# A two-layer network on one core: layer 1's last attention product and feed forward by token tile, five weight-quantising operations instead of one, and a new set of scheduling tables

## Chip, cores and metric

The kernel runs on one NeuronCore of a Trainium2 chip. The time is that of the device for one launch, in microseconds (us), as the median of several executions; with one core there is no slowest one to choose. The engines are TensorE (PE in the profile: matmuls, with its weight loads listed as PEld), VectorE (DVE), ScalarE (ACT), GpSimd (POOL) and SyncE (SP). SyncE does no arithmetic here: it issues all the DMA transfers, also the transposing ones.

## The reference, cut to what matters

The input `x` is 64 sequences of 64 tokens with 256 features each, so 4096 tokens; `ctx_2048` has the same shape. Six blocks are added to `x` one after the other, each from a layer-normalised `x`:

```python
x = x + L0_attn(layernorm(x))          # 16 heads, 4 shared K/V heads, 128 wide, rotary, causal
x = x + L0_xattn(layernorm(x), ctx)    # 8 heads; features attend to features
x = x + L0_ffn(layernorm(x))           # base product + one of 8 low-rank experts for each token
x = x + L1_attn(layernorm(x))          # 16 heads of 16, one shared K/V head, causal
x = x + L1_xattn(layernorm(x), ctx)    # 16 heads of 128, RMS-normalised q and k
x = x + L1_ffn(layernorm(x))           # 8 bit SwiGLU, 704 wide
```

The two blocks that the change touches, cut to their core:

```python
# L1_xattn
q = rms_norm(x @ q_w + q_b, nq_s);  k = rms_norm(ctx @ ki_w + ki_b, nki_s);  v = ctx @ vi_w + vi_b
out = softmax(q k^T / sqrt(128)) v            # per head, 64 x 64 in each sequence
return out @ o_w + o_b

# L1_ffn
def _quant_dequant(v):                        # per row
    scale = max(max|v| / 127, 1e-8)
    return clip(round(v / scale), -127, 127) * scale
gate, up = split(_quant_dequant(x) @ _quant_dequant(w_gate_up)^T)
h = silu(gate) * up
return _quant_dequant(h) @ _quant_dequant(w_down)^T
```

## The kernel before, in words

**Tiling.** The 4096 tokens go in 16 groups of 256 (`GT`). A group is held as an array `xt` of 128 partitions by 2 token tiles by 256 features; index `j` counts the token tiles. Layer 0 (called phase a: the blocks a0, x0, f0) is done for a group, the result goes to DRAM (`mid`), and layer 1 (phase b: a1, x1, f1) reads it back. Phase a of later groups and phase b of earlier ones are in flight together around the middle of the run.

**The order.** No loop of the text sets the order in which the engines get their instructions. The text of each block records operations: `s.o(engine, cost, reads, writes, function)`, and `s.alt` where two engines may do it. One operation can issue several instructions of one engine, and those then stand together. When all are recorded, a planner (`Sched.plan`) goes through them as a list scheduler on its own cost figures. An operation has a due time: a target that comes from the phase's pace (`PACE`, `SHIFT`), plus an entry of `LEAD` for the block and the name of the tile, plus an entry of `FINE` for its place in the group. Among the operations that could start on an engine at about the same time (`EPS`), the one with the earliest due time is taken. `HOLD` is added to the due time of a TensorE operation that would change the tile mode (the part of the array that a matmul uses: 128x128, 128x64, 128x32 or 32x128), `PEN` counts against a choice where VectorE would take an operation that another engine could take, `WINDOW` is how many groups of each phase may be open, `SPACE` sets the least distance between the score steps of x0, and `TMIN` the earliest starts of setup operations. The planned order is emitted as straight code, engine by engine: each engine then runs its own list in order, and waits at the semaphores of what it needs. A planned order is thus fixed when the kernel is built; the planned times are not.

**Memory.** Tiles come from pools by size: `B` (8 banks of PSUM, 2 KB a partition), `k4` (6 buffers of 4 KB), `k2` (67 of 2 KB), `k1` (6 of 1 KB), `sm` (10 small ones).

**Lines that the change and the prediction speak of.**

- Helpers: `layer_norm` (L555 statistics, L557 aggregation, L562 and L566 small GpSimd steps, L569 the normalising on ScalarE); `dma_T` (L578, a transposing DMA of a whole tile); the three-term product of split f16 numbers (L430 to L432); `softmax_rows` (L625 to L655: maxima, differences, exponentials, sums, the split `phl`).
- a0: query products `q_ps`, sums of squares `ss` (L881), scores `s_ps` (L933) with a mask and scale step (L935, L937), `po` products from the transposed `pt` (L689), the split `ohl` (L694, L696), output product `acc`.
- x0: `stack_rows` sends rows through DRAM into `ovl` (the issues `hl_d` and `ovl`), `xs_ps` scores (L1033), maxima `xmx` (L1040), `mx_ps` and `mneg` (the maxima are transposed and sent through DRAM as one more row), `xt_ps` scores again in the other orientation (L1067), exponentials `xpt` (L1074), `xo_ps` (L1083), the sum at L1113.
- f0: `f0o_ps` (L1167). a1: `q1st` rows sent through DRAM, `s_ps` (L1312), `pT` transposes and the context product (L1327).
- x1 (`l1_xattn`): q and k products `qk_ps` with biases (L1650), scores `s_ps` (L1662). Its heads go in two halves of eight; for each, `value_block` makes `vn` = context times a product of value and output weights (`vn_ps` L1541; ScalarE takes the high half L1546, VectorE the low half L1548), and `attend_rows` multiplies the probabilities into it.
- `attend_rows`: for both token tiles a transposing DMA of `phl` to `pt` and 24 matmuls into one PSUM tile `acc` of 128 x 2 x 256 (L1564); then one VectorE instruction adds `acc` times a scale to the whole `xt` (L1568).
- f1 weights (`l1_ffn_prep`, once, at the start of phase b): five chunks, each a load `f_w` (L1693), one VectorE operation of six instructions (L1699 the row maximum, L1677 and L1678 the scale and its reciprocal, L1701 the multiplication, L1702 and L1703 the rounding by adding and subtracting a large number), TensorE transposes `fw_ps` (L1712), a ScalarE copy `f_t` (L1715) and stores to DRAM (L1719).
- f1 (`l1_ffn`): layer norm, row maximum `f1am` (L1764), scale `f1sx` (L1765) and its reciprocal `f1ix` (L1766), each one instruction for both token tiles; rounding per token tile (L1768, L1770); one transposing DMA for both, `xqT`; then per token tile four products `gu_ps` of two matmuls (L1784) scaled out of PSUM by VectorE (L1786), ScalarE's `sig` (L1789), GpSimd's gate product (L1791), the second quantisation (L1799 to L1812), the transposing DMA `hqT`, the product `f1o_ps` (L1819), its scaling (L1822) and GpSimd's addition into `xt` (L1825). One DMA writes the group's output (L2081).

Of the kernel before, what the change touches and what calls it, by code (L numbers as in the profile page):

```python
# [11 lines left out]
BF16 = mybir.dt.bfloat16  # L12
# [7 lines left out]
D = 256  # L20
# [16 lines left out]
HOLD = 965  # L37
# [1514 lines left out]
def attend_rows(e, xt, phl, vn, uo):  # L1552


    nc, s = e.nc, e.s
    acc = s.T("B", [128, 2, D], name="acc")
    for j in range(2):
        pt = s.T("k2", [128, 8, 128], F16, name="pt")
        dma_T(e, phl[j], pt, lambda t: t.rearrange("p a h l -> p (a h l)"))

        def f(t, h0, l0, h1, l1, o, j=j):
            for n, (p, a, c) in enumerate((p, a, c) for p in range(4) for a, c in ((0, 0), (0, 1), (1, 0))):
                for b in range(2):
                    nc.tensor.matmul(o[64 * b:64 * b + 64, j, :], t[:, 4 * a + p, 64 * b:64 * b + 64],  # L1564
                                     ((h0, l0), (h1, l1))[b][c][:, p, :], start=(n == 0), stop=(n == 11))
        s.o("PE", 12 * 110, [pt] + list(vn[2 * j] + vn[2 * j + 1]), [acc.sub(j)], f, tile=3)
    s.o("DVE", c_dve(512, 1), [acc, uo], [xt],
        lambda a, u, x: nc.vector.scalar_tensor_tensor(x, a, u, x, ALU.mult, ALU.add))  # L1568
# [112 lines left out]
def l1_ffn_prep(e, I):  # L1681
# [4 lines left out]
    for nm, src, nr, n, per in (("gu", I["w_gu"], 11, 256, 4), ("dn", I["w_dn"], 2, 704, 1)):  # L1686
# [3 lines left out]
        for a0 in range(0, nr, per):  # L1690
# [7 lines left out]
            def f(t, am, iv, sc, b, a0=a0, na=na, n=n):  # L1698
                nc.vector.tensor_reduce(am, t, AX.X, ALU.max, apply_absolute_value=True)  # L1699
                row_scale(nc, sc[:, a0:a0 + na], iv, am)  # L1700
                nc.vector.tensor_tensor(t, t, bc(iv, 2, n), ALU.mult)  # L1701
                nc.vector.tensor_scalar(t, t, MAGIC, None, ALU.add)  # L1702
                nc.vector.tensor_scalar(b, t, MAGIC, None, ALU.subtract)  # L1703
            s.o("DVE", 3.2 * na * n + 500, [t], [am, iv, sc.sub(a0), b], f)
# [50 lines left out]
def l1_ffn(e, xt):  # L1755
# [3 lines left out]
    xh = layer_norm(e, xt, 1.0)  # L1759
    am, sx, ix = (s.T("sm", [128, 2], name="f1" + n) for n in ("am", "sx", "ix"))  # L1760
    xq = s.T("k1", [128, 2, D], BF16, name="xq")

    V = nc.vector
    s.o("DVE", c_dve(512), [xh], [am], lambda x, am: V.tensor_reduce(am, x, AX.X, ALU.max, apply_absolute_value=True))  # L1764
    s.o("DVE", Port(130), [am], [sx], lambda am, sx: V.tensor_scalar(sx, am, 1.0 / 127, 1e-8, ALU.mult, ALU.max))  # L1765
    s.o("DVE", Port(140), [sx], [ix], lambda sx, ix: V.reciprocal(ix, sx))  # L1766
    for j in range(2):
        s.o("DVE", c_dve2(256, 1), [ix], [xh.sub(j)], lambda ix, x, j=j: V.tensor_scalar(  # L1768
            x[:, j, :], x[:, j, :], ix[:, j:j + 1], MAGIC, ALU.mult, ALU.add))
        s.o("DVE", c_dve2(256), [xh.sub(j)], [xq.sub(j)], lambda x, q, j=j: V.tensor_scalar(  # L1770
            q[:, j, :], x[:, j, :], MAGIC, None, ALU.subtract))
    xqT = s.T("k1", [128, 4, 128], BF16, name="xqT")
    dma_T(e, xq, xqT, lambda t: t.rearrange("p j n -> p (j n)"))
    ah, s2, sh, ih = (s.T("sm", [128, 2], name="f1" + n) for n in ("ah", "s2", "sh", "ih"))
    for j in range(2):

        gu = [s.T("k4", [128, 2, HI], name="gu") for _ in range(2)]
        for a in range(4):
# [6 lines left out]
            s.o("PE", 303, [xqT, w.gu], [ps], f)  # L1785
# [3 lines left out]
        s.o("ACT", c_act(704, 1), [gu[0], sx], [sig], lambda g, a, t, j=j: nc.scalar.activation(  # L1789
# [12 lines left out]
        s.o("DVE", Port(120), [sx], [s2.sub(j)], lambda x, s2, c=c: V.tensor_tensor(s2[:, c], x[:, c], x[:, c], ALU.mult))  # L1802
# [42 lines left out]
def ctx_scale(e, I, nt):  # L1845
# [16 lines left out]
PEN = 247.38  # L1862
NQ = 1
LEAD = {
    ".xt": -7500, "a0.acc": 6500, "a0.bias_ps": -16000, "a0.bm": -112500, "a0.k_ps": -6000, "a0.kf": -4000,
    "a0.ku": -27000, "a0.ln_mv": 86500, "a0.ln_nb": -120000, "a0.ln_rs": 43000, "a0.ln_st": 60500, "a0.nr_v": -2500,
    "a0.nr_y": -92000, "a0.ohl": -35000, "a0.phl": -9500, "a0.po": -500, "a0.pt": 36500, "a0.qu": -2500,
    "a0.rb": 21500, "a0.rk": 2000, "a0.s1": -4500, "a0.s_ps": -27500, "a0.sm_mx": 120000, "a0.sm_sm": -2500,
    "a0.sq": -2000, "a0.ss": 15500, "a0.ss_t": -7000, "a0.sss": 30500, "a0.sw": 38000, "a0.v_ps": -50000,
    "a0.vt": 84000, "a0.vx": 111500, "a0.xT": -26500, "a0.xh": 112500, "a0.xhl": -29000, "a0.xt": -3000,  # L1870
    "a1.ctx1": -38500, "a1.k1": -120000, "a1.k1_ps": -24500, "a1.ksh": 26000, "a1.kst": -32000, "a1.ln_mv": 96000,
    "a1.ln_nb": -55000, "a1.ln_rs": 68500, "a1.ln_st": 120000, "a1.o1_ps": 47500, "a1.oT1": 23000, "a1.pT": -31000,
    "a1.phl": -101000, "a1.q1": 119500, "a1.q1_d": -9500, "a1.q1_ps": -56500, "a1.q1hl": 26500, "a1.q1st": 120000,
    "a1.s1": 120000, "a1.s1_ps": -90500, "a1.sm_f": -3000, "a1.sm_mx": -76000, "a1.sm_sm": 104000, "a1.v1": 90000,
    "a1.vbd": 10500, "a1.xT": 37000, "a1.xh": -8500, "a1.xhl": -6000, "a1.xt": 73500, "f0.-": -112500,
    "f0.f0_ps": -19500, "f0.f0o_ps": -14500, "f0.hT": -69000, "f0.hm": -120000, "f0.hm_ps": 20500, "f0.ln_mv": -4000,
    "f0.ln_nb": 39000, "f0.ln_rs": 42000, "f0.ln_st": 52000, "f0.xT": 78000, "f0.xh": 24000, "f0.xhl": -18000,
    "f0.xt": -11000, "f1.f1ah": 114500, "f1.f1am": -13000, "f1.f1ix": -115500, "f1.f1o": -116500, "f1.f1o_ps": -4500,
    "f1.f1s2": 73500, "f1.f1sx": 81500, "f1.gu": 8500, "f1.gu_ps": -112500, "f1.hq": -53500, "f1.hqT": 93500,
    "f1.ln_mv": 81500, "f1.ln_nb": -116500, "f1.ln_rs": -3000, "f1.ln_st": 31000, "f1.sig": 32000, "f1.xh": -10500,  # L1880
    "f1.xq": -119500, "f1.xqT": 111000, "f1.xt": 30500, "setup.-": 15500, "setup.a1am": 100500, "setup.am_ps": -4000,
    "setup.bo_ps": 70500, "setup.bo_w": -46500, "setup.cen": -72500, "setup.ctx_a": 64000, "setup.ctxa1": 99000,
    "setup.f_t": -94500, "setup.f_w": 23000, "setup.fam": -23500, "setup.fw_ps": 40000, "setup.g_G": -68500,
    "setup.g_ps": -75500, "setup.g_w": -21000, "setup.l0cols": 87500, "setup.l0ek": 7500, "setup.l0eq": -32500,
    "setup.l0w0": -3500, "setup.l0w1": -120000, "setup.l0w2": 67000, "setup.l0w3": 14000, "setup.l0w4": 96000,
    "setup.n_am1": 11500, "setup.n_o": -60000, "setup.n_ps": -116500, "setup.n_v": 120000, "setup.n_w": -28500,
    "setup.nf": 31500, "setup.p2_ar": -85500, "setup.p2_p2": -64500, "setup.rope_t": -34000, "setup.rp_tmp": -49000,
    "setup.sqj": -80000, "setup.w_a1": -25000, "setup.w_a1o": -110500, "setup.w_am1": -59000, "setup.w_f0": -77500,
    "setup.w_hl": -18500, "setup.w_l0kv": 7000, "setup.w_l0o0": -4000, "setup.w_l0o1": -7500, "setup.w_l0q0": -77000,
    "setup.w_l0q1": 26000, "setup.w_n": 47000, "setup.w_x1ki0": -30500, "setup.w_x1ki1": -15500,  # L1890
    "setup.w_x1q0": -64500, "setup.w_x1q1": 14500, "setup.x1wki0": 18500, "setup.x1wki1": 116500,
    "setup.x1wn0": 33500, "setup.x1wn1": 41000, "setup.x1wn2": 77500, "setup.x1wn3": 56000, "setup.x1wq0": 25500,
    "setup.x1wq1": -93500, "setup.xtwo": -62500, "x0.-": -120000, "x0.cT": -11500, "x0.ctx": 9000, "x0.hl": -82000,
    "x0.hl_d": -42500, "x0.ln_mv": -10000, "x0.ln_nb": -71000, "x0.ln_rs": -118000, "x0.ln_st": -103000,
    "x0.mneg": -99500, "x0.mx_ps": -37500, "x0.so": -80000, "x0.xh": 24500, "x0.xmx": -105500, "x0.xo_ps": 3500,
    "x0.xot_ps": 49500, "x0.xpt": 13500, "x0.xrc": -17500, "x0.xs_ps": -16500, "x0.xt": -41000, "x0.xt_ps": 2500,
    "x0.y": -35000, "x0.yo": -82500, "x1.acc": -38000, "x1.cTs": -120000, "x1.chl": 68500, "x1.ctx": -50000,
    "x1.gac": 42000, "x1.gjk": -34000, "x1.gy_ps": 48000, "x1.k8": -29500, "x1.ln_mv": 74500, "x1.ln_nb": -119500,
    "x1.ln_rs": -55000, "x1.ln_st": 87000, "x1.ms": -111500, "x1.phl": 6000, "x1.pt": 64000, "x1.q8": -90000,
    "x1.qk_ps": 17500, "x1.rkL": 103000, "x1.rkb": -88500, "x1.rkb_ps": -49000, "x1.rms": 24500, "x1.s1": 120000,  # L1900
    "x1.s_ps": -120000, "x1.sm_mx": -22000, "x1.sm_sm": -68500, "x1.vn": 117000, "x1.vn_ps": 68000,
    "x1.x1esc": -45000, "x1.xT": 88000, "x1.xh": 116000, "x1.xhl": 117000, "x1.xt": 23500,
}
RESV = 1e+15
TMIN = {"setup.w_a1": 1457, "setup.w_l0kv": -4579, "setup.w_x1q1": 1916, "setup.x1wki1": -18878, "setup.x1wn0": 1785, "setup.x1wn2": -1297, "setup.x1wn3": -2931, "setup.x1wq1": -2255}
# [282 lines left out]
```

## Time and profile before

The three executions took 2370.43, 2370.53 and 2375.34 us; their median is 2370.53. The profiled execution took 2375.9 us, of which the span from the first to the last instruction is 2374.1.

| what | us | from |
|---|---|---|
| median of the runs | 2370.5 | times |
| profiled execution, span in it | 2375.9, 2374.1 | times, page |
| value products `vn_ps`, 6144 matmuls | 357.9 | groups, L1541 |
| scores of x0, `xmx` on VectorE, 512 | 316.5 | groups, L1040 |
| exponentials of x0, `xpt` on ScalarE, 512 | 316.2 | groups, L1074 |
| `phl` on GpSimd, 192 | 221.9 | groups, L655 |
| last `acc` products, 1536 matmuls | 95.4 | groups, L1564 |
| gate and up products scaled on VectorE, 128 | 57.8 | groups, L1786 |
| gate product on GpSimd, 32 | 55.5 | groups, L1791 |

Times are busy time of one group of instructions. A row of the group table gives the line, the engine, the operation, output and input tiles with their shapes, the number of instructions, then busy us, the mean ns of one, the idle time of the engine just ahead of them, and after `<-` what ended most of it. A row of the timeline gives the start and the length in us of one instruction or a few like it, and in brackets how long the engine had waited and for what. In a row of the waits the numbers are the summed us, how often, and the longest. A row by stretch gives the bounds and the length of a stretch, then for PE, PEld, DVE, ACT and POOL the busy us with the number of instructions, the mean granted clock of TensorE (1.00 is full speed), the busy share of the DMA engines and the GB/s that they moved.

### The profile page before, as it was taken

How to read it: one execution, taken by the hardware profiler on the slowest of the kernel's cores; microseconds unless marked ns; L12 is line 12 of the kernel's file. 1: busy time of each engine (PE TensorE's matmuls, PEld its weight loads, DVE VectorE, ACT ScalarE, POOL GpSimd, SP SyncE). 2: the span in 40 equal slices, each digit the busy share in tenths (PEclk: the TensorE clock that was granted, in tenths of full speed). 3: DMA queues.
4: the chain of work that ended last, by engine and by line, in shares of the span. 5: the costliest groups of instructions: out<-in, count | busy, mean ns of one | idle time of the engine just before them, and what ended most of it. 6: DMA issues, size and time to landing. Idle time of an engine off the chain costs nothing. (4 is left out here: it accounts for less than half of the span.)

```text
span 2374.1 us, 69674 instructions
## 1 busy us (share of the span) xinstructions
PE 2168.2 (91%) x28232; PEld 1692.0 (71%) x28232; DVE 1828.7 (77%) x4256; ACT 1594.2 (67%) x3047; POOL 1691.1 (71%) x1793
## 2 busy tenths in 40 slices
PE   6887889988898978999988999999999999999996
PEld 5765556655565645666645788898888988889885
DVE  7577689877878778788887766778877777777766
ACT  7864878777677768788767675666566655656552
POOL 6897898776857677688945664677777667667642
PEclk9997999999899999999989999999999999999997
DMA  7744444342344234244353353444434444343322
GB/s 233 231 118 104 113 110 115 99 110 64 99 112 95 60 62 90 47 114 104 75 157 77 73 108 66 78 86 77 77 79 78 74 81 83 77 79 77 64 33 41
DMA packets 484322, 220.82 MB, mean 93 GB/s; under 512 B 340568, under 2 KB 463384, under 8 KB 484000
## 3 DMA queue, kind: packets, MB, share of 16 engines
q1 hardware_dynamic: 484000, 216.37, 40.1%
q8 instruction: 222, 3.64, 0.6%
q14 instruction: 100, 0.82, 0.1%
HBM read 89.06 MB, written 34.64 MB: 52 GB/s over the span
## 5 line engine op out<-in xcount | busy, mean ns | idle before, releaser
L1541 PE MATMUL vn_ps<-x1wn,cTs 128*64 128x256 f16 x6144 | 357.9, 273 | 0.5 <-ACT q L1282 0.5
L1074 ACT ACTIVATE xpt<-xt_ps,xes 128x512 f32<-128x512 f32 x512 | 316.2, 699 | 61.8 <-PE xt_ps L1067 56.1
L1541 PEld LDWEIGHTS <-cTs 128*64 128x64 f16 x6144 | 327.1, 110 | 17.0 <-issue 15.1
L1040 DVE TENSOR_REDUCE xmx<-xs_ps 128x2 f32<-128x512 f32 x512 | 316.5, 679 | 27.5 <-PE xs_ps L1033 27.0
L626 POOL TENSOR_TENSOR s<-s,sm_mx 128x1024 f32<-128x1024 f32 x96 | 183.6, 1913 | 196.1 <-DVE sm_mx L625 118.3
L1546 ACT ACTIVATE vn<-vn_ps 128x512 f16<-128x512 f32 x256 | 149.2, 593 | 137.8 <-PE vn_ps L1541 136.2
L1548 DVE SCALAR_TENSOR_TENSOR vn<-vn_ps,vn 128x512 f16<-128x512 f32 x256 | 170.7, 680 | 87.2 <-ACT vn L1546 86.7
L655 POOL TENSOR_TENSOR phl<-s,phl 128x512 f16<-128x512 f32 x192 | 221.9, 1166 | 17.7 <-ACT phl L654 13.4
L652 POOL TENSOR_TENSOR s<-s,sm_sm 128x512 f32<-128x512 f32 x192 | 201.5, 1062 | 7.2
L835 POOL TENSOR_TENSOR sw<-sw,rp0s 128x512 f32<-128x512 f32 x128 | 164.8, 1296 | 15.1 <-ACT sq L833 12.9
L654 ACT CAST phl<-s 128x512 f16<-128x512 f32 x192 | 118.4, 620 | 81.5 <-POOL s L652 80.9
L832 ACT COPY sw<-q_ps 64x512 f32<-64x512 f32 x256 | 146.9, 579 | 32.0 <-PE q_ps L432 24.4
L837 POOL TENSOR_TENSOR qu<-qu,sw 128x512 f32<-128x512 f32 x128 | 163.4, 1283 | 2.0
L1650 ACT ACTIVATE k<-qk_ps,x1kb 128x256 f32<-128x256 f32 x240 | 100.6, 471 | 95.1 <-PE qk_ps L432 94.8
L1083 PE MATMUL xo_ps<-xpt,xve 128*32 128x256 f32 x2048 | 150.6, 404 | 7.9 <-ACT xpt L1074 6.1
L569 ACT ACTIVATE xh<-xt,ln_nb,ln_rs 128x256 f32<-128x256 f32 x192 | 107.2, 599 | 61.2 <-POOL ln_nb L566 60.8
L430 PE MATMUL q_ps<-xT,l0w 128*128 128x256 f16 x512 | 140.8, 275 | 2.0 <-ACT mneg L1044 0.8
L430 PE MATMUL acc<-l0w,ohl 128*128 128x256 f16 x512 | 141.2, 276 | 0.5 <-DVE ohl L696 0.4
L432 PE MATMUL q_ps<-xT,l0w 128*128 128x256 f16 x512 | 140.4, 274 | 0.7 <-DVE l0w L541 0.7
L431 PE MATMUL acc<-l0w,ohl 128*128 128x256 f16 x512 | 141.0, 275 | 0.0
L432 PE MATMUL acc<-l0w,ohl 128*128 128x256 f16 x512 | 140.9, 275 | 0.1
L430 PE MATMUL qk_ps<-cTs,x1wki 128*128 128x256 f16 x512 | 140.8, 275 | 0.0
(416 smaller groups left out, 6697.8 us busy)
## 6 DMA issues: line engine op xcount, KB each, us to landing
ovl<-hl_d SPq DMA_DIRECT2D x96, 128.0 KB
vx<-vt SPq DMA_DIRECT2D x64, 128.0 KB
ctx<-in_ctx_dram SPq DMA_DIRECT2D x32, 256.0 KB
hl_d<-hl SPq DMA_DIRECT2D x64, 128.0 KB
wd<-w_hl SPq DMA_DIRECT2D x32, 256.0 KB
q1st<-q_d SPq DMA_DIRECT2D x128, 64.0 KB
xt<-in_x_dram SPq DMA_DIRECT2D x16, 256.0 KB
ctx_a<-in_ctx_dram SPq DMA_DIRECT2D x8, 512.0 KB
```

The costliest lines, as they stand in the source:

```text
L430: nc.tensor.matmul(out, lh, rh, start=(st and i == 0), stop=False, **kw)
L432: nc.tensor.matmul(out, ll, rh, start=False, stop=(i == n - 1), **kw)
L626: s.o("POOL", 1900, [mx], [s1], lambda m, t: nc.gpsimd.tensor_tensor(t, t, bc(m, 2, 64), ALU.subtract))
L652: s.o("POOL", 1030, [sm], [s1.sub(j)], lambda m, t, h=h: nc.gpsimd.tensor_tensor(t[:, h], t[:, h], bc(m[:, h], 2, 64), ALU.mult))
L655: s.alt([("POOL", c_pool(482), lambda t, _, p, h=h: nc.gpsimd.tensor_tensor(pl(p, 1), t[:, h], pl(p, 0), ALU.subtract)), ("DVE", c_dves(51 ...
L835: s.o("POOL", 1225, [sg], [sw], lambda t, w: nc.gpsimd.tensor_tensor(v(w), v(w), bc(t, 1, 8), ALU.mult))
L837: ("POOL", 1225, lambda w, d: nc.gpsimd.tensor_tensor(view(d), view(d), w, ALU.add))], [sw], [dt])
L1040: nc.vector.tensor_reduce(m[:, h, bs % 4, :], p, AX.X, ALU.max))
L1074: nc.scalar.activation(t, p, AF.Exp, scale=a))
L1083: nc.tensor.matmul(o[32 * hh:32 * hh + 32, hs, :], v[:, n, a:a + 32], r[hh][:, n, :], start=(n == 0 and hs == 0), stop=(n == 1), skip_grou ...
L1541: nc.tensor.matmul(r[-1][64 * h:64 * h + 64, p, :], x[:, b // 2, a, k, t], w.part(r, c, 2 * (2 * p + h) + k), start=(n == 0), stop=(n == 5))
L1548: nc.vector.scalar_tensor_tensor(v(l), p, 2.0 ** -15, v(h), ALU.mult, ALU.subtract))
```

## The change

The text changes in four places, and the values that the planner works from change:

1. `attend_rows`: each token tile has its own PSUM tile `acc` of 128 x 256 and its own multiply-add into its half of `xt`.
2. `l1_ffn_prep`: the one operation of six VectorE instructions becomes five operations (the two instructions of `row_scale` stay together), which the planner places one by one.
3. `l1_ffn`: the layer norm is written out per token tile, as are the maximum, the scale, its reciprocal and the transposing DMA of `xq` to `xqT`; what reads them waits for its own token tile alone.
4. The output of a group is written by two DMAs, one for each token tile.
5. `HOLD`, `PEN`, `SPACE`, `SHIFT`, phase b's `PACE`, `WINDOW` and the tables `LEAD`, `TMIN` and `FINE` have new values. `PACE` of phase a stays.

The matmuls, 24,485 of them as instructions, are the same in kind and number. The number of tile mode turns in TensorE's list goes from 1064 to 1012.

```diff
-HOLD = 965
+HOLD = 789
...
-    acc = s.T("B", [128, 2, D], name="acc")
     for j in range(2):
+        acc = s.T("B", [128, D], name="acc")
         pt = s.T("k2", [128, 8, 128], F16, name="pt")
         dma_T(e, phl[j], pt, lambda t: t.rearrange("p a h l -> p (a h l)"))
...
-        s.o("PE", 12 * 110, [pt] + list(vn[2 * j] + vn[2 * j + 1]), [acc.sub(j)], f, tile=3)
-    s.o("DVE", c_dve(512, 1), [acc, uo], [xt],
-        lambda a, u, x: nc.vector.scalar_tensor_tensor(x, a, u, x, ALU.mult, ALU.add))
+        s.o("PE", 12 * 110, [pt] + list(vn[2 * j] + vn[2 * j + 1]), [acc], f, tile=3)
+        s.o("DVE", c_dve(256, 1), [acc, uo], [xt.sub(j)], lambda a, u, x, j=j: nc.vector.scalar_tensor_tensor(
+            x[:, j, :], a, u, x[:, j, :], ALU.mult, ALU.add))
...
-            def f(t, am, iv, sc, b, a0=a0, na=na, n=n):
-                nc.vector.tensor_reduce(am, t, AX.X, ALU.max, apply_absolute_value=True)
-                row_scale(nc, sc[:, a0:a0 + na], iv, am)
-                nc.vector.tensor_tensor(t, t, bc(iv, 2, n), ALU.mult)
-                nc.vector.tensor_scalar(t, t, MAGIC, None, ALU.add)
-                nc.vector.tensor_scalar(b, t, MAGIC, None, ALU.subtract)
-            s.o("DVE", 3.2 * na * n + 500, [t], [am, iv, sc.sub(a0), b], f)
+            s.o("DVE", c_dve(na * n), [t], [am], lambda t, am: nc.vector.tensor_reduce(
+                am, t, AX.X, ALU.max, apply_absolute_value=True))
+            s.o("DVE", 230, [am], [iv, sc.sub(a0)], lambda am, iv, sc, a0=a0, na=na: row_scale(
+                nc, sc[:, a0:a0 + na], iv, am))
+            s.o("DVE", c_dves(na * n), [iv], [t], lambda iv, t, n=n: nc.vector.tensor_tensor(t, t, bc(iv, 2, n), ALU.mult))
+            s.o("DVE", c_dve2(na * n), [], [t], lambda t: nc.vector.tensor_scalar(t, t, MAGIC, None, ALU.add))
+            s.o("DVE", c_dve2(na * n), [t], [b], lambda t, b: nc.vector.tensor_scalar(b, t, MAGIC, None, ALU.subtract))
...
-    xh = layer_norm(e, xt, 1.0)
-    am, sx, ix = (s.T("sm", [128, 2], name="f1" + n) for n in ("am", "sx", "ix"))
...
+    xqT = s.T("k1", [128, 4, 128], BF16, name="xqT")
     for j in range(2):
+        c = slice(j, j + 1)
+        s.o("DVE", 336, [xt.sub(j)], [st.sub(j)], lambda x, t, j=j: V.bn_stats(t[:, j, :], x[:, j, :]))
+        s.o("DVE", 108, [st.sub(j)], [mv.sub(j)], lambda t, m, j=j: V.bn_aggr(m[:, j, :], t[:, j, :]))
...
+        s.o("ACT", c_act(D, 2), [xt.sub(j), nb.sub(j), rs.sub(j)], [xh.sub(j)], lambda x, b, r, h, j=j, c=c:
+            nc.scalar.activation(h[:, j, :], x[:, j, :], AF.Identity, scale=r[:, c], bias=b[:, c]))
+        s.o("DVE", c_dve(256), [xh.sub(j)], [am.sub(j)], lambda x, am, j=j, c=c: V.tensor_reduce(
+            am[:, c], x[:, j, :], AX.X, ALU.max, apply_absolute_value=True))
...
-    xqT = s.T("k1", [128, 4, 128], BF16, name="xqT")
-    dma_T(e, xq, xqT, lambda t: t.rearrange("p j n -> p (j n)"))
+        s.o("SP", DMA_NS + 400, [xq.sub(j)], [xqT.sub(j)], lambda x, t, j=j: nc.sync.dma_start(
+            t[:, 2 * j:2 * j + 2], x[:, j], transpose=True), TR_NS)
...
-            s.o("PE", 303, [xqT, w.gu], [ps], f)
+            s.o("PE", 303, [xqT.sub(j), w.gu], [ps], f)
...
-SPACE = (7285, 2674)
+SPACE = (6464, 2691)
...
-SHIFT = -31810.49
+SHIFT = -9659.09
...
-PACE = dict(a=(81129.88, 2.24), b=(66158.31, 2.05))
+PACE = dict(a=(81129.88, 2.24), b=(65562.85, 1.68))
...
-WINDOW = (5, 6)
+WINDOW = (4, 6)
...
-            s.o("SP", DMA_NS + 1400, [xt], [], lambda t: nc.sync.dma_start(e.tok(out, g), t))
+            for j in range(2):
+                s.o("SP", DMA_NS + 700, [xt.sub(j)], [], lambda t, j=j: nc.sync.dma_start(e.tok(out, g)[:, j], t[:, j]))
```

## The prediction, made before the changed kernel had run

> **What bounds the kernel now.** I read the page first, then the busy time by stretch, then the waits, then the timeline at the places they name. All from the profiled execution: span 2374.1 us, 2375.9 us with what lies around it.
>
> ```profile
> span 2374.1 us, 69674 instructions
> ...
> PE 2168.2 (91%) x28232; PEld 1692.0 (71%) x28232; DVE 1828.7 (77%) x4256; ACT 1594.2 (67%) x3047; POOL 1691.1 (71%) x1793
> ...
> PEclk9997999999899999999989999999999999999997
> ```
>
> TensorE is the busiest engine at 91%, and its granted clock falls only in the first 60% of the span and in the last slice. So its losses are not spread evenly. I cut the span at the first vn_ps product (1323.1 us) and at the last acc product (2341.9 us); columns are length, busy us of each engine, clock, DMA share, GB/s.
>
> ```profile
> 0.00:1323.10 1323.10, 1150.77 (x12955) 793.03 (x12955) 1038.25 (x2475) 973.80 (x1801) 1009.90 (x1006) 0.94 0.43 108
> 1323.10:2341.90 1018.80, 1007.13 (x15240) 893.84 (x15239) 772.00 (x1736) 617.53 (x1242) 672.70 (x776) 1.00 0.39 75
> 2341.90:2374.10 32.20, 10.29 (x41) 5.14 (x40) 18.43 (x47) 2.85 (x4) 8.53 (x12) 0.58 0.20 46
> ```
>
> Stretch A (0 to 1323): TensorE idles 172 us and loses about another 59 us to half clock (the clock rows put 119 us of its busy time there at half speed); no other engine passes 78%. This is layer 0 with the setups: chains of short steps between engines. Stretch B: 1007 of 1019 us busy at full clock, so layer 1 is TensorE's work itself. Stretch C, 32.2 us, is the last group's feed forward, a chain that nothing hides.
>
> TensorE's matmuls are the same 24,485 instructions in both kernels, so the change can save only idle, half clock, and tile-mode turns.
>
> **The change, part by part.** The instruction lists of the two built kernels tell what stands where.
>
> *Stretch A, how much stands in it.* Ahead of the first vn_ps product stand 10,264 matmuls, 2,472 VectorE, 1,736 ScalarE and 1,006 GpSimd instructions before; after the change 10,218, 2,474, 1,736 and 988. The new order does not move work out of A, and I price the amount at 0. What changes are waits.
>
> *The five quantisation operations.* One block of six VectorE instructions a chunk, five chunks, becomes separately placed instructions. Two things cost time at it now.
>
> ```profile
> 726.03 3.62 DVE L1677 TENSOR_SCALAR fsc<-fam 128x4 f32<-128x4 f32 x1
> ...
> 734.33 0.37 PE L1067 MATMUL xt_ps<-ovl 32*128 32x256 f16 x5 [3.11 <-DVE s L935]
> ...
> 865.00 0.89 DVE L1699 TENSOR_REDUCE fam<-f_w 128x1 f32<-128x704 f32 x1 [7.53 <-DMA f_w<-in_w_dn_dram]
> ...
> 868.38 0.29 PE L1712 MATMUL fw_ps<-identb,f_b 128*128 128x128 bf16 x1 [7.40 <-DVE f_b L1703]
> ```
>
> VectorE runs in order: at 865 it had waited 7.53 us for weights issued at 852.5, and TensorE stood 7.40 us behind it; from 869.0 to 876.5 the clock was 0.55, and 6.22 us of busy time there did about 3.3 us less. At 724.8 the block held VectorE 8.8 us, and TensorE idled 3.11 us for the score step behind it. At 673.8 it idled 1.54 us. Together 7.4 + 3.3 + 3.1 + 1.5 = 15.3 us. In the new list the fourth chunk has 148 matmuls and 24 VectorE instructions between its load and its maximum (30 and 6 before), the first 92 and 6 (33 and 3), and 10 to 28 VectorE instructions stand between maximum and last step (6 before). At 109 ns a matmul of the commonest form, 148 are up to 16 us against the 12.5 us from issue to use at 852.5. I take -15. Bounds: 0 if the new order waits elsewhere, -25 if the 3.62 us step and its followers in the other chunks shrink too.
>
> *Tighter transfers in A.* For each wait of TensorE for a transfer I summed the matmuls (start to start) between the transfer's place in the list and the wait. Under 2.5 us stood 84 before, 121 after: xs_ps (L1033, rows of K and Q) 1 to 18, xt_ps (L1067, the row of maxima) 3 to 17, layer 1's s_ps (L1312) 20 to 36, projections from xT 12 to 18; po (L689) falls 22 to 15, f1o_ps 15 to 2; the rest nets -2. What one tight wait costs now:
>
> ```profile
> PE po L689 <- DMA pt<-phl: 11.1, 13, 2.2
> ...
> PE s_ps L1312 <- DMA q1st<-q_d: 4.2, 4, 2.2
> ```
>
> 4.2 / 20 = 0.21 us for rows passed through DRAM, 11.1 / 22 = 0.50 for transposes. 37 more at 0.21 is +8; most are rows of the first kind, so I take +8. Bounds 0 (the 15 tight f1o_ps waits cost nothing until the tail) and 37 x 0.50 = +18.
>
> *Stretch B, the turns.* A switch of TensorE between tile modes has its next matmul start 205 ns after the last instead of 109, so 0.096 us. In the built order 298 turns stand after the first vn_ps product before and 234 after; in the steady cycle 17 a group become 12. 64 x 0.096 = -6.1. The 46 matmuls that moved out of A into B add 3.0 at their rows. Sum -3. The smaller acc (one 128x256 bank a tile) and halved multiply-adds (one 128x512 at 739 ns becomes two near the 410 ns of the 128x256 row at L1113) and the doubled small GpSimd steps lie under TensorE: VectorE is 76% and GpSimd 66% busy in B. Without that cover the multiply-adds alone cost 32 x 0.08 = 2.6 us.
>
> SyncE gets 16 transposes and 16 output writes more: 16 x 1.19 + 16 x 0.40 = 25 us of issue over B, hidden. The new wait is the second xqT transpose, which stands ahead of the four pT transposes of the next group; the ctx products wait for those. gu_ps now waits for xqT twice a group; 4 of these 32 waits are tight, 1 of 16 before, and are counted above. The five exposed ones of B cost 0.46 to 0.84 us each. If every second half were exposed at 0.5: +8, kept for the range.
>
> The Trainium skill speaks against this piece: "DMA: Bandwidth & Descriptors", Rules for kernel authors, says to coalesce transfers because under 64 KB one pays mostly overhead. By its figure of about 2.0 us fixed a transfer, 16 exposed halves would be an estimated +32 us. The rows here show the transposes hidden in 11 of 16 groups.
>
> *Stretch C.* Lines that set it:
>
> ```profile
> 2343.05 0.75 DVE L1568 SCALAR_TENSOR_TENSOR xt<-acc,x1uo,xt 128x512 f32<-128x512 f32 x1
> ...
> 2350.70 1.19 SPq L578 DMA_TRANSPOSE xqT<-xq  x1
> ...
> 2353.15 4.53 PE L1784 MATMUL gu_ps<-ovl,xqT 128*128 128x352 bf16 x16 [4.54 <-DMA xqT<-xq]
> 2353.96 4.42 DVE L1786 TENSOR_TENSOR gu<-gu_ps,ovl 128x352 f32<-128x352 f32 x8 [3.14 <-PE gu_ps L1784]
> ```
>
> After the change tile 0 is through its feed forward's first half when tile 1's acc ends. Tile 1 saves: the 1.1 us wait of its multiply-add behind the other group's hq steps, half of stats, multiply-add, normalising, maximum and rounding (0.33 + 0.37 + 0.5 + 0.27 + 0.8 = 2.3), and the eight gu products ahead of it (2.3 at half clock). Against that, VectorE reaches tile 1's rounding only behind tile 0's gate product, which waits for a 1.68 us GpSimd multiply: +0.7. Sum -5; bounds -8 and -1.
>
> **Sum.** -15 + 8 - 3 - 5 = -15. The profiled execution took 2375.9, 5.4 above the median 2370.5 of the runs shown; carried to the median: 2370.5 - 15 = 2355.5, I say 2355. Added up, the bounds give -38 to +20 (with the +8); what the reordering does to the other 215 us lost in A no row tells.
>
> **Rivals.**
> *Slower: the rows for layer 0's scores arrive late.* In A, xs_ps and xt_ps lose their cover. If a tight wait costs more than (15 + 3 + 5) / 37 = 0.62 us, the gain is gone; at 1.0 us, between the 0.50 above and the 2.2 us longest wait, it is +37 - 23 = +14, so 2385. For: 172 us of idle in A are just such chains, no engine saturated. Against: xs_ps waits for a transfer hardly at all now.
> *Much faster: A tightens as a whole.* From 960 to 1140 TensorE was busy 167.8 of 180 us at full clock, 7% lost; from 285.7 to 1198.3 it idled 98 and lost 34 to the clock of 913, 14%. If half of that excess goes, -33 more: 2322. For: the amounts in A are equal, so only waits separate the stretches. Against: nothing in the list singles it out.
> *Nothing:* the quantisation's idle comes back at the next late chain (the amounts stay, VectorE has 78% to do either way): -15 becomes 0, then 0 + 8 - 8 = 0: 2371.
>
> **How the numbers follow.** Forecast 0.53 (its own range 2340 to 2365), much faster 0.14, nothing 0.08, slower 0.25. No change means within 0.2%, 4.7 us, about what a measurement of this kernel can tell. Faster 0.67, same 0.08, slower 0.25. The range 2322 to 2388 reaches the fast rival's time and just past the slow one's.
>
> **What would show it.** Right: no VectorE wait over 3 us at the five maxima and no TensorE gap at fw_ps over 2 us; a B period of about 64.3 us (64.75 now); 27 us from the last acc to the end; first vn_ps near 1316. Wrong: first vn_ps later than 1331, with xs_ps or xt_ps at the head of TensorE's waits for transfers; or gu_ps waiting in every group.

## The result and the profile after

The changed kernel took 2431.16 us (median of four executions, 2427.21 to 2439.53), the kernel before 2372.94 beside it (2370.43 to 2377.25). The ratio is 1.025, with a 95% interval of 1.0227 to 1.0273: 58 us slower, where 15 less had been forecast and the range ended at 2388.

The page of the profiled execution of the changed kernel, as it was shown of before:

```profile
span 2425.4 us, 69843 instructions
...
PE 2181.9 (90%) x28232; PEld 1703.1 (70%) x28232; DVE 1837.5 (76%) x4328; ACT 1613.4 (67%) x3086; POOL 1702.6 (70%) x1812
...
PEclk9998888999999989999998999999999999999998
```

Nothing stands out: TensorE is busy for 14 us more over a span that is 51.3 us longer, and each of the other engines for 9 to 19 us more. The row of the clock differs in a few slices of layer 0. So I cut the span at the same two products as before. The first vn_ps product starts at 1369.7 (1323.1 before), the last acc product ends at 2398.2. Columns as in the prediction:

```profile
0.00:1369.70 1369.70, 1172.11 (x12918) 799.80 (x12920) 1055.06 (x2474) 970.29 (x1802) 990.71 (x986) 0.93 0.40 103
1369.70:2398.20 1028.50, 1002.87 (x15289) 900.13 (x15288) 768.57 (x1820) 640.88 (x1281) 705.37 (x818) 1.00 0.42 77
2398.20:2425.40 27.20, 6.88 (x29) 3.19 (x28) 13.91 (x35) 2.25 (x3) 6.55 (x9) 0.57 0.12 27
```

Stretch A is 46.6 us longer (1369.7 against 1323.1), B 9.7 longer (1028.5 against 1018.8), C 5.0 shorter (27.2 against 32.2). The sum, 51.3, is the whole difference of the spans. A holds the same work: 12,918 recorded matmuls against 12,955, 2474 VectorE instructions against 2475. TensorE's idle time in it went from 172 to 198 us, its busy time from 1151 to 1172. Most of this second rise is half clock: the clock rows put 141 us of TensorE's busy time in A at half speed, 112 before (the prediction's 119 hold 7 that lie just behind the cut), and 29 us more at half speed do 15 us less.

Which waits changed? First before, some of TensorE's waits in its stretch A; columns are the us in total, the times, the longest:

```profile
PE ss L881 <- ACT sq L833: 13.7, 7, 6.8
...
PE fw_ps L1712 <- DVE f_b L1703: 8.9, 2, 7.4
...
PE s_ps L933 <- POOL kf L911: 6.1, 7, 2.2
...
PE xt_ps L1067 <- ACT xpt L1074: 6.0, 17, 1.8
...
PE xs_ps L1033 <- DVE xmx L1040: 4.1, 8, 1.7
PE xot_ps L1095 <- ACT so L1088: 4.1, 7, 0.9
...
PE rk L905 <- POOL rb L899: 0.6, 1, 0.6
```

The same view of the changed kernel, in its stretch A:

```profile
PE s_ps L933 <- POOL kf L911: 12.9, 12, 3.5
PE xt_ps L1067 <- ACT xpt L1074: 12.1, 25, 2.7
PE xot_ps L1095 <- ACT so L1088: 11.7, 15, 1.5
...
PE rk L905 <- POOL rb L899: 10.1, 8, 5.0
PE po L689 <- DMA pt<-phl: 9.0, 8, 2.1
PE xs_ps L1033 <- DVE xmx L1040: 8.2, 11, 4.0
...
PE ss L881 <- ACT sq L833: 3.5, 5, 2.4
```

The waits that grew are links of one group's own chain (key norms, scores, maxima, exponentials, the transposes behind them), each waiting for the step ahead of it on another engine. Others shrank, the sums of squares `ss` and the weight transposes `fw_ps` most. Added up over all lines, TensorE's waits in A for VectorE rose from 61.0 to 81.0 us and those for GpSimd from 17.3 to 33.1. Its waits for ScalarE fell from 58.0 to 54.0, those for transfers from 31.9 to 24.6. I read this as no new bottleneck, but less other work to put between two steps of a chain.

That can be counted. In TensorE's list of the built kernel, take for each point the number of groups whose first matmul has been issued and whose last one has not, and average it over TensorE's work. In the middle of layer 0 this gives 4.6 for the kernel before and 3.7 for the changed one; in layer 1 it gives 4.5 and 3.5. That agrees with the entry WINDOW of the diff, 5 to 4. Its two numbers are not one for each layer, as the description of the order had it: in the planner (L288) the first one limits the open groups of both layers together, the second those of layer 1 alone. So the step from 5 to 4 narrows both layers, and the 6 never binds.

### The profile page after: what moved, and what is told of

The parts are those of the page before. It is cut to its first block, busy times and chain, and to the rows that moved or that the text cites. A ratio compares the mean times of both kernels' runs of the same rounds, so it can differ in the third digit from the quotient of the medians.

```text
span 2425.4 us, 69843 instructions
## 1 busy us (share of the span) xinstructions
PE 2181.9 (90%) x28232; PEld 1703.1 (70%) x28232; DVE 1837.5 (76%) x4328; ACT 1613.4 (67%) x3086; POOL 1702.6 (70%) x1812
## 4 chain that ended last, share of the span: by engine, by line
PE 43%; POOL 18%; DVE 12%; ACT 10%; DMA 9%; issue 6%; SPq 1%; POOLq 0%; DVEq 0%; ACTq 0%
PE vn_ps L1541 8%; ACT xpt L1074 3%; PE qk_ps L430 3%; PE qk_ps L432 3%; PE qk_ps L431 3%; DVE xmx L1040 3%; PE acc L1564 3%; POOL phl L655 3%; POOL s L652 2%; DMA pt<-phl 2%; POOL sw L835 2%; POOL s L626 2%; ACT sw L832 2%; PE s_ps L1662 2%; PE xo_ps L1083 2%
## 5 line engine op out<-in xcount | busy, mean ns | idle before, releaser
L1040 DVE TENSOR_REDUCE xmx<-xs_ps 128x2 f32<-128x512 f32 x512 | 317.1, 680 | 33.2 <-PE xs_ps L1033 33.1
L1650 ACT ACTIVATE k<-qk_ps,x1kb 128x256 f32<-128x256 f32 x254 | 106.2, 469 | 138.6 <-PE qk_ps L432 137.5
L1083 PE MATMUL xo_ps<-xpt,xve 128*32 128x256 f32 x2048 | 158.1, 411 | 7.7 <-ACT xpt L1074 7.0
L1650 ACT ACTIVATE q<-qk_ps,x1qb 128x256 f32<-128x256 f32 x250 | 104.7, 471 | 61.1 <-PE qk_ps L432 55.0
```

The source lines that it names most:

```text
L1040: nc.vector.tensor_reduce(m[:, h, bs % 4, :], p, AX.X, ALU.max))
L1083: nc.tensor.matmul(o[32 * hh:32 * hh + 32, hs, :], v[:, n, a:a + 32], r[hh][:, n, :], start=(n == 0 and hs == 0), stop=(n == 1), skip_grou ...
L1650: nc.scalar.activation(d[:, c, :], p[:, c, :], AF.Identity, bias=b[:, b0 + c:b0 + c + 1])
```

## The experiments

**How an order is held.** The planner reacts to any change of an input with another order, so a part of the change can't be undone by editing one line. In the first four runs and in e11 the order is therefore fixed. The planner ran once more with the planned starts of a given kernel as its only due times (HOLD and PEN 0), and the order that came out was written into the kernel as a table:

```diff
-        for o in self.plan():
+        for o in map(self.ops.__getitem__, ORDER):
...
-            o.fn(*[t.parent.real for t in o.R + o.W])
+            next(f for e, _, f in o.alts if e == TAKES.get(o.idx, e))(*[t.parent.real for t in o.R + o.W])
```

A run is named old or new by its text (parts 1 to 4 of the change) and by its order. Ratios are against the kernel before on the same chip.

### e1, the control: old text, old order

> The text of before, its order planned once more with the planned starts of before as the only due times (no extra for a tile mode turn, five groups open) and written into the kernel. It shows what the replanning itself costs: on average 4.6 groups have TensorE work begun and unfinished in layer 0 (4.6 before), 1081 tile mode turns (1064 before). Both theories: the time of before, 2371 +- 8 us.

Measured: 2385.09 us, ratio 1.0041 (1.0024 to 1.0059). That lies 6 us above the interval of both theories. Planning once more at the same depth costs 0.4%, 11 us: so much the placing of single steps is worth. The next three runs are to be read against it.

### e2, new text in the old order

> All four text changes, but in the order of before (planned as in e1, a split operation due when the joint one was; the small tiles of the feed forward have a pool of their own, without which five groups do not find room). 4.6 groups open in layer 0. Theory one, the loss is the order, with 3.7 instead of 4.6 groups open: the text alone gives what was forecast for quantisation and tail, 15 + 5 us off the control, so 2345 to 2370. Theory two, the text itself costs (more transposes, more small steps): 2415 or more, as the changed kernel.

The text is that of the changed kernel, with a pool `ss` of eight buffers for the feed forward's tiles of 8 bytes:

```diff
-    rs, nb, am, sx, ix = (s.T("sm", [128, 2], name=n) for n in ("ln_rs", "ln_nb", "f1am", "f1sx", "f1ix"))
+    rs, nb, am, sx, ix = (s.T("ss", [128, 2], name=n) for n in ("ln_rs", "ln_nb", "f1am", "f1sx", "f1ix"))
...
-    ah, s2, sh, ih = (s.T("sm", [128, 2], name="f1" + n) for n in ("ah", "s2", "sh", "ih"))
+    ah, s2, sh, ih = (s.T("ss", [128, 2], name="f1" + n) for n in ("ah", "s2", "sh", "ih"))
```

Measured: 2387.81 us, ratio 1.0055 (1.003 to 1.0081). The text itself costs nothing that can be told from the control, but it gives none of the forecast 20 us either; the value lies above the first theory's interval. In the profiles the parts show: first vn_ps 1335.1 (control 1335.8), from the start of the last acc product to the end 27.4 us (32.3), and 2.9 us more between these two points.

### e3, old text in the new order

> The text of before in the order of the changed kernel (its planned starts as due times, four groups open; 3.7 open in layer 0). Theory one: as slow as the changed kernel or slower, since the gains of the text are missing: 2425 to 2450. Theory two: near before, 2370 to 2385.

Measured: 2438.7 us, ratio 1.0253 (1.0227 to 1.0279). With none of the four text changes it is as slow as the changed kernel. First vn_ps stands at 1378.2, 42 us behind the control. So the order lost the time, with either text: 54 us in the old one (2438.7 against 2385.1), 43 in the new one (2431.2 against 2387.8). In the second pair only e2 has paid for the planning once more; with its 11 us the new text comes to 54 too.

### e4, the five operations alone

> The text of before with only the quantisation block in five operations, these and the chunks' loads placed where the changed kernel has them, all else in the order of the control. The forecast's term: 15 us less than the control, about 2356, without the 7.4 us gap at the weight transposes. Rival: the other work moves up into the same stalls and the time is that of the control, within 5 us.

Measured: 2385.49 us, ratio 1.0054 (1.0034 to 1.0074): nothing against the control. TensorE's waits in the control:

```profile
PE f_ps L430 <- DMA xT<-xhl: 18.7, 5, 12.7
...
PE mx_ps L1042 <- DVE xmx L1040: 6.6, 6, 2.4
...
PE fw_ps L1712 <- DVE nr_y L614: 6.0, 1, 6.0
```

and in e4, where fw_ps has none left:

```profile
PE mx_ps L1042 <- DVE xmx L1040: 11.1, 6, 5.5
...
PE xs_ps L1033 <- ACT sss L887: 5.7, 1, 5.7
PE f_ps L430 <- DMA xT<-xhl: 5.3, 4, 1.9
```

The 6.0 us at the weight transposes and a 12.7 us wait for xT, both in the control, are gone. In their place stand waits that the control doesn't have, 5.7 us at xs_ps for a ScalarE step and 5.5 at the transposing of the maxima. In the stretch to 1330 us TensorE idles 178.0 us, in the control 178.6. VectorE's longest wait for a chunk's weights is not gone by the split: it is 6.3 us here and 5.4 in the control. The first vn_ps starts at 1330.2, 5.6 us ahead of the control's, but the control's profile is of the slowest of its ten executions (2390.3), so this tells nothing.

### e5 and e6, five groups or four, without fitted tables

In the runs so far two fitted orders are compared; whether their depth makes the difference or their detail, they don't tell. So the tables were emptied, and only WINDOW differs:

```diff
-LEAD = {
...
-TMIN = {"setup.w_a1": 1457, "setup.w_l0kv": -4579, "setup.w_x1q1": 1916, "setup.x1wki1": -18878, "setup.x1wn0": 1785, "setup.x1wn2": -1297, "setup.x1wn3": -2931, "setup.x1wq1": -2255}
-FINE = dict(a=[
...
+LEAD = {}
+TMIN = {}
+FINE = dict(a=[], b=[])
...
-WINDOW = (5, 6)
+WINDOW = (4, 6)
```

The last two lines are in e6 alone.

> The text of before with the three tables LEAD, TMIN and FINE emptied, so that no order was fitted to it, and five groups open as before: 4.4 groups have TensorE work begun and unfinished in layer 0 and in layer 1. It is the base for the next run. Slower than before, since the tables are gone; by how much no row tells: 2400 to 2500 us.

> As the run before it, but four groups open (WINDOW (4, 6)); 3.7 have TensorE work begun and unfinished. Theory: the number of open groups is what the changed kernel lost by. If a group's way through a layer took as long as with five, the rate would fall by 4.4 / 3.7, so up to 19% of some 2300 us, 430; with fewer groups each one waits less for the engines, so I expect 100 to 250 us more than with five. Rival: only the fitted details of the order matter, and the two plain orders lie within 30 us.

Measured: 2461.53 us with five (ratio 1.0399, 1.0352 to 1.0446), 2606.51 with four (1.1011, 1.0954 to 1.1069). One group less in flight costs 145 us, 5.9%, with every other value of the planner the same. The page of e5, span and engines:

```profile
span 2461.9 us, 69795 instructions
...
PE 2207.8 (90%) x28232; PEld 1695.7 (69%) x28232; DVE 1864.4 (76%) x4299; ACT 1585.8 (64%) x3019; POOL 1692.5 (69%) x1767
```

and of e6:

```profile
span 2601.0 us, 69785 instructions
...
PE 2257.7 (87%) x28232; PEld 1727.2 (66%) x28232; DVE 1880.1 (72%) x4291; ACT 1592.6 (61%) x3012; POOL 1700.0 (65%) x1787
```

ScalarE and GpSimd are busy for nearly the same time, and every engine's share falls: the signature of too little work in flight. Of TensorE's 50 us more of busy time some 36 are half clock (257 us of its busy time at half speed against 184; mean granted clock 0.930 against 0.947).

The stretch ahead of the first vn_ps tells more. With five groups, then with four:

```profile
0.00:1363.10 1363.10, 1163.87 (x12630) 784.05 (x12631) 1037.81 (x2438) 956.42 (x1755) 996.51 (x988) 0.92 0.41 103
```

```profile
0.00:1409.30 1409.30, 1180.74 (x12650) 794.46 (x12650) 1040.81 (x2435) 946.30 (x1741) 984.83 (x981) 0.91 0.38 99
```

WINDOW alone makes it 46.2 us longer for the same work, as much as stretch A grew in the changed kernel (46.6). The other 93 us lie behind it; of them the fitted order of the changed kernel shows almost nothing (5 us from there to the end).

### e7, e8 and e12: the new text and its small tiles

> The text of the changed kernel, its three tables emptied and five groups open; its other values kept. Theory: by token tile, the feed forward holds its small tiles from the first token tile's start to the second one's end, and the pool of ten does not take five groups any more; the planner then falls to 1.5 open groups in layer 1, and the time is several hundred us above the old text's. Rival: the new text does as well as the old one with five open, 2400 to 2500.

> As the run before it, but nine small tiles of the feed forward (8 bytes a partition each) have a pool of their own with ten buffers. 4.4 groups are open in layer 0, 4.2 in layer 1. Theory: the time falls back to that of the old text with five open, within 60 us. Rival: the text itself is slow, and the pool changes little.

> The changed text with its three tables emptied and its own four open groups (3.7 in layer 0, 3.3 in layer 1), beside the run with five and the additional pool, 2470. Theory: what four groups cost the old text (145 us) they cost the new one too, 2560 to 2640. Rival: for the new text four are no worse than five, 2450 to 2490.

e8 differs from e7 by the lines of the pool, as in e2, here with ten buffers; e12 differs from e7 by WINDOW = (4, 6). Measured: e7 3076.84 us (ratio 1.2998, 1.2945 to 1.3051), e8 2470.09 (1.0435, 1.0392 to 1.0478), e12 2554.06 (1.0754, 1.0711 to 1.0797). The page of e7, with TensorE's row of busy tenths:

```profile
span 3074.2 us, 70183 instructions
...
PE   6988888888888999799974846747647557467397
```

Up to slice 21 TensorE is as busy as in the other runs. Then, in layer 1, it falls to some 65%, and a group takes 121 us (from one group's last gate and up product to the next one's) instead of 65 in the changed kernel. Written by token tile, the feed forward holds seven small tiles (ln_mv, ln_st, ln_rs, ln_nb, f1am, f1sx, f1ix) from the first token tile's statistics to the second one's rounding, where the old text frees the four of the layer norm once both tiles are normalised; four more follow. The pool `sm` has ten buffers for all groups. With ten further buffers in a pool of their own, 80 bytes a partition, the new text with five groups is where the old one is (2470 and 2462). With four groups and the old pool it takes 84 us more than that; its 2554 lie just under the interval of the theory. The two ran on different chips; by the ratios it is 76, and the pool differs too. All of it lies ahead of the first vn_ps, which starts at 1410.1 in e12 and at 1325.7 in e8; from there to the end the two take 1146.3 and 1143.4 us. So in this text the lower depth costs time in layer 0 and next to none in layer 1.

So the new text does not fit five groups into the pools, and four groups cost some 80 to 145 us before any table is fitted. That WINDOW was set to 4 for this reason is inferred; that five don't go with this text and these pools, and what four cost, is measured. What a fitted order loses by WINDOW alone was not tried: the 43 to 54 us above hold the depth and all that the new tables place otherwise.

### e9, the quantisation left out

> The kernel before in its own order; the five quantisation blocks are left out but for one copy to 8 bit exact numbers' type (the weights are not scaled or rounded), the instructions of the scale and a constant maximum, so VectorE holds each chunk for some 1.5 us instead of 8.8. It bounds from above what any placement of the five operations can bring. The forecast's term: at least 15 us less than before, the 7.4 us gap at the weight transposes and the gaps of 3.1 and 1.5 us gone. Rival, after the run in which the split alone gave nothing: these gaps go, others take their place, and the gain is under 8 us.

```diff
-                nc.vector.tensor_reduce(am, t, AX.X, ALU.max, apply_absolute_value=True)
+                nc.vector.memset(am, 1.0)
                 row_scale(nc, sc[:, a0:a0 + na], iv, am)
-                nc.vector.tensor_tensor(t, t, bc(iv, 2, n), ALU.mult)
-                nc.vector.tensor_scalar(t, t, MAGIC, None, ALU.add)
-                nc.vector.tensor_scalar(b, t, MAGIC, None, ALU.subtract)
+                nc.vector.tensor_copy(b, t)
```

Measured: 2360.4 us against 2371.78, ratio 0.9956 (0.9938 to 0.9974), so 11 us less (6 to 15), between the two expectations. This is what the blocks cost where they stand. It does not bound what a placement can bring that also issues the loads earlier, as the changed kernel's does: the wait that I had called the largest stall of the block is still there, first TensorE's, then VectorE's waits in this run:

```profile
PE fw_ps L1712 <- DVE f_b L1701: 5.8, 1, 5.8
```

```profile
DVE f_b L1701 <- DMA f_w<-in_w_dn_dram: 8.3, 1, 8.3
```

The copy at L1701 stands where the block stood, and it waits 8.3 us for the weights. Set against this run, some 5.8 of the 7.40 us at fw_ps in the kernel before were the late load and 1.6 the block behind it.

### e10, one transpose more

> The kernel before in its own order, with the transposing DMA of xq to xqT issued as two, one behind the other, in its place: 16 DMAs more on SyncE, nothing else. In the run with the new text in the old order, the context product waited 6.1 us for pT in ten groups (1.0 in the control) and a group took 65.4 us (64.9). Theory: the additional transpose, ahead of pT on SyncE's queue, is the cause; the period rises by 0.4 to 0.6 us, the time by 6 to 10, with the context product at the head of TensorE's waits in layer 1. Rival: it is the place of the second transpose in that order and not its number; then no change within 3 us.

```diff
-    dma_T(e, xq, xqT, lambda t: t.rearrange("p j n -> p (j n)"))
+    s.o("SP", DMA_NS + 700, [xq], [xqT], lambda x, t: [nc.sync.dma_start(t[:, 2 * j:2 * j + 2], x[:, j], transpose=True) for j in (0, 1)], TR_NS)
```

Measured: 2372.91 us against 2371.78, ratio 1.0002 (0.9986 to 1.0019). The interval, -3 to +5 us, excludes the theory's 6 to 10: a second transpose in the place of the first costs nothing that can be told.

### e11, the new text with five groups

> The changed text with the pool of its own for the feed forward's small tiles and five groups open, as in the run with the new text in the old order, its due times moved by small steps over some thousand planned orders, and the best of them written into the kernel: 4.65 groups open in layer 0, 1061 tile mode turns. Theory: with five groups open nothing in the text stands against the time of before, and the tail's 5 us come on top: 2340 to 2370, under both kernels. Rival: a planned order does not carry over to the chip by less than 1%, and it stays at the 2388 of its starting point.

Measured: 2366.48 us against 2374.43 for the kernel before, ratio 0.9969 (0.9954 to 0.9983): 0.3% faster than it, and 65 us faster than the changed kernel with the same text but for the pool. First vn_ps 1318.5, end of the span 28.9 us after the last acc began. This is the fastest complete kernel of the study. Its gain over e2, 21 us, came from the order alone, at nearly the same depth and with the same pools, so the place of single steps counts too, with less than half of what the changed kernel's order cost (43 to 54 us).

## Why the prediction was wrong

**"The new order does not move work out of A, and I price the amount at 0. What changes are waits."** This is the step that failed. The count of instructions ahead of the first vn_ps was right and says nothing about how many groups they belong to. I had listed the new WINDOW in the change and gave it no price. In the changed kernel, with one open group less, A is 46.6 us longer; in e3, where the order alone is new, 42; in e6, where WINDOW alone is new, 46 against e5. It shows in no single wait: none of TensorE's in A grew by more than 10 us.

**The quantisation, -15.** Its stalls went as forecast. In the changed kernel VectorE waits for the chunks' loads and TensorE for the weights no longer than this, first the one, then the other:

```profile
DVE fam L1698 <- DMA f_w<-in_w_dn_dram: 2.2, 1, 2.2
...
DVE fam L1698 <- DMA f_w<-in_w_gu_dram: 0.7, 1, 0.7
```

```profile
PE fw_ps L1712 <- DVE f_b L1704: 1.1, 1, 1.1
```

The time did not follow: 0 in e4, and 11 us if the blocks are left out (e9). The stall that I counted as 7.4 us of the block was for the most part the late load (e9), and the 3.3 us for the clock behind it were 2.8 (6.22 us at 0.55). The sum of stalls was taken for a gain. The rival "nothing" had named what happens instead: the idle time comes back at the next late chain. It held for this term; the rest of that rival did not come.

**Tighter transfers, +8.** Wrong in sign. TensorE's waits for transfers in A fell by 7 us; those of xs_ps and xt_ps for their rows are 4.4 us together. Counting matmuls between a transfer and its use measured the wrong resource: what lost its cover were the steps of VectorE and GpSimd (+20 and +16 us). The slower rival had the right direction, but for this wrong reason; it put 14 us on rows that came in time. The list of tight waits in the prediction also adds up to 31 more, not 37.

**Stretch B, -3.** It is 9.7 longer. The turns fell as counted, from 17 to 12 in a group; the period rose from 64.75 to 65.7 us. TensorE's waits in ten groups (1500 to 2150 us) were 5.4 us in all before; the four longest are now:

```profile
PE qk_ps L430 <- DMA cTs<-chl: 6.4, 7, 1.8
PE ctx L1327 <- DMA pT<-phl: 3.0, 2, 1.6
PE s_ps L1312 <- DMA q1st<-q_d: 2.9, 8, 0.5
PE acc L1564 <- DMA pt<-phl: 1.9, 4, 0.6
```

The same stretch of e3, old text in the new order, has three of the four:

```profile
PE qk_ps L430 <- DMA cTs<-chl: 5.5, 7, 1.6
PE s_ps L1312 <- DMA q1st<-q_d: 3.5, 8, 0.5
PE acc L1564 <- DMA pt<-phl: 1.5, 2, 1.3
```

and that of e2, new text in the old order, has another one:

```profile
PE ctx L1327 <- DMA pT<-phl: 6.1, 7, 1.3
```

So the order, with 3.5 groups open in place of 4.5, brings the first, the third and the fourth, and the text the second. From the first vn_ps to the last acc, e3 takes 5.8 us more than the control and e2 2.9 more, which together is near the 9.7. For the wait that I had named as new, pT behind the second xqT transpose, I had kept +8 for the range. In e2 it appears where it was said to, 6.1 us in ten groups, so some 10 us in sixteen; as e10 shows, the number of transposes doesn't make it. That its place does, behind the second token tile's rounding, was not tried by itself. The Trainium skill's rule to coalesce ("DMA: Bandwidth & Descriptors", Rules for kernel authors) spoke against splitting; a half is 128 x 256 x 2 bytes, 64 KB, at the edge of that rule. By the page's figure of about 2.0 us fixed, which its section "Anatomy of one DMA — SWDGE (gpsimd) path" gives for transfers that GpSimd issues, 16 exposed transfers would have been an estimated 32 us. Here SyncE issues them, and the 16 transposes more cost nothing measurable (e10).

**Stretch C, -5.** Right: 27.2 us against the 27 forecast, and, from the start of the last acc product, 27.4 in e2 against 32.3 in the control. The timeline of the changed kernel shows it:

```profile
2398.30 0.48 DVE L1567 SCALAR_TENSOR_TENSOR xt<-acc,x1uo,xt 128x256 f32<-128x256 f32 x1 [0.80 <-PE acc L1564]
...
2398.87 1.37 PE L1798 MATMUL gu_ps<-ovl,xqT 128*128 128x352 bf16 x8 [0.61 <-DMA xqT<-xq]
...
2405.11 0.28 DVE L1784 TENSOR_SCALAR xq<-xh 128x256 bf16<-128x256 f32 x1
...
2407.74 2.53 PE L1798 MATMUL gu_ps<-ovl,xqT 128*128 128x352 bf16 x8 [7.50 <-DMA xqT<-xq]
```

Tile 0's gate and up products run at 2398.9, right behind the last acc; tile 1 reaches its own at 2407.7, 9.5 us after the products ended (before, both tiles together at 2353.15, 11.3 us after).

In sum: A forecast -7, measured +46.6; B -3 and +9.7; C -5 and -5.0. The bounds of the terms, added up with the +8, give -36 to +22 and not the -38 to +20 of the prediction; +58 lies far outside either, since none of them holds a term for the depth.

## What to carry to other kernels

Where a scheduler interleaves several groups, count the groups in flight before and after a change, and look at whatever limits them (a window, a pool of small buffers): the depth is a resource like an engine, and losing one group of five cost 3 to 6% here in orders without fitted tables, without one conspicuous wait (ahead of the first vn_ps in both texts, behind it in one of them). A stall that is removed is a gain only if the work behind it is not late at the next place; leaving the suspected work out shows in one run what it costs where it stands. And before splitting a step in two, see how long its scratch tiles now live: 80 bytes a partition decided over 600 us.

## What the hardware showed unexpectedly

A transposing DMA of half a tile keeps SyncE as long as one of a whole tile (1.17 us for one xqT at L1786 after, 1.19 at L578 before), and still sixteen more of them in the queue cost nothing that can be told (e10, 1.1 us with an interval that holds 0). I take this to be because SyncE's queue had the room: between 1500 and 2150 us its transfers' issues fill 40% of the time before and 42% in e10. TensorE's granted clock was lower with four groups than with five, where the work is the same: 0.930 against 0.947 in e6 and e5, 0.944 against 0.959 in e12 and e8.
